# Moving the squares, the row sums and the cast of the high halves from VectorE to ScalarE in the last stage of a four-layer graph network

## The chip, the cores and the metric

The kernel runs on one core of a Trainium2 chip. Its time is the device time in microseconds of one execution; the figure used is the median over several executions. The profile is a separate, profiled execution, which takes longer than the others. Engines are named as in the profile: PE is TensorE's matmul, PEld its weight load, DVE is VectorE, ACT is ScalarE, POOL is GpSimd, SP is SyncE; ACTq and SPq are the queues on which ScalarE and SyncE issue DMAs.

## The reference, cut to what matters

The network has 6250 nodes with 128 features and 106250 edges (`src`, `dst`), and four layers, each with a layer norm and a Relu ahead and a residual sum behind. The change lies in the last of them, which is itself three graph layers:

```python
def _l2norm(v):
    n = jnp.linalg.norm(v, axis=-1, keepdims=True)
    return v / jnp.maximum(n, EPS)          # EPS = 1e-12
...
denom = jnp.maximum(cnt, 1.0)               # cnt: edges that end in each node
for i in range(NUM_LAYERS):                 # 3
    msg = x[src]
    agg = jax.ops.segment_sum(msg, dst, num_segments=N) / denom
    agg = _l2norm(agg)
    out = agg @ Wl[i].T + bl[i]
    out = out + _l2norm(x) @ Wr[i].T
    x = jax.nn.relu(out) if i != NUM_LAYERS - 1 else out
```

Each graph layer sums the rows of the neighbours, divides by the in-degree, scales the sum and the node's own row to length one, multiplies both with a 128x128 matrix, and adds.

## The kernel before, in words

The nodes are padded to 49 tiles of 128. At the start the kernel builds the adjacency (how many edges run from a source to a destination) as one byte for each pair in DRAM; a sum over neighbours is then a dense matmul with that matrix. Destinations are handled in 13 blocks of up to 512 nodes (the last has 128).

`aggregate` (lines 262 to 284) makes the sums of one block. For each group of up to four source tiles it loads the bytes (`ra_in`, three buffers, on SyncE's queue), casts them to fp32r into `ra_r` (two buffers in the last stage), and multiplies. The cast is shared: VectorE casts the first two or three source tiles of a group (L274), ScalarE the rest (L276). The features are kept as a high and a low fp32r half, so each source tile takes two matmuls (L279). The features stand in `cur` (fp32, called `rh` in the profile) and in `cur2` and `other` (both halves, written in turn by alternate layers).

The stage before the last walks over the edges. While it runs, it also sums most of the source tiles for the first graph layer (L1071), into `part`; for that layer, l=0, only the last 5 of 49 source tiles are left to the last stage (`late`). Layers l=1 and l=2 sum all 49.

The last stage (lines 1163 to 1233) loops over l and the 13 blocks. For each block:

- The sum is copied out of PSUM: L1184 on ScalarE, or L1186 on VectorE for l=0, where `part` is added. This gives `ag` (`rag`), features by nodes.
- L1188 squares it on VectorE into `sq` (`rsq`, one buffer). `transposed` makes `hT` (`rhT`) from the node's own rows by four transposes (L291) and a copy on ScalarE (L292).
- For each of the four node tiles there are three small matmuls: L1196 sums the squares over the features, L1197 multiplies `ag` with `Wl`, L1198 `hT` with `Wr`. In the profile each counts as two.
- `n1` (L1201, L1202) and `rsqrt_clipped` (clip L252 on VectorE, Sqrt L254 on ScalarE, reciprocal L255 on VectorE) give the factor `s1` of the aggregate (L1205).
- L1207 and L1209, both on VectorE, square the block's own rows into `r` (`rr`, one buffer) and sum each row into `n2`; this depends on nothing else in the block. `rsqrt_clipped` gives `s2`.
- L1213, L1215, L1217 and L1219 form the output `o` on VectorE, with `r` used again for the second product.
- For l=0 and l=1, L1221 writes Relu(o) to `cur`; `split_halves` then casts it into the high half (L259) and subtracts that for the low half (L260), all on VectorE. For l=2 the residual `rxb` is added (L1226) and the rows are stored; the load of `rxb` (L1225) and the store (L1229) are issued on ScalarE's queue.

No order is written out by hand. A scheduler orders the instructions of each engine when the kernel is built, from priorities that follow the program and from its own estimate of when operands are ready; on the chip each engine then runs its queue in that order. TensorE's queue may therefore hold matmuls of the next block's sum ahead of the small matmuls of this one.

Of the kernel before, what the change touches and what calls it, by code (L numbers as in the profile page):

```python
# [14 lines left out]
AF = mybir.ActivationFunctionType  # L15
ALU = mybir.AluOpType
AX = mybir.AxisListType
# [39 lines left out]
def blk_tiles(b):  # L57
    return min(4, NT - 4 * b)
# [17 lines left out]
def bcast_rows(ap, off, n):  # L76
    return bass.AP(tensor=ap.tensor, offset=ap.offset + off, ap=[[0, P], [1, n]])
# [56 lines left out]
def regular_path(ctx: ExitStack, tc: tile.TileContext, i: dict, out: bass.AP):  # L134

    nc = tc.nc
# [112 lines left out]
    def rsqrt_clipped(dst, n2, n):  # L249

        c = small.tile([P, 4], F32, name="rrq_c")
        nc.vector.tensor_scalar(c[:, :n], n2, 1e-24, None, op0=ALU.max)  # L252
        s = small.tile([P, 4], F32, name="rrq_s")
        nc.scalar.activation(s[:, :n], c[:, :n], AF.Sqrt)  # L254
        nc.vector.reciprocal(dst, s[:, :n])  # L255

    def split_halves(hi, lo, x):

        nc.vector.tensor_copy(hi, x)  # L259
        nc.vector.tensor_tensor(lo, x, hi, ALU.subtract)  # L260

    def aggregate(b, pool, psum, rows2, t0, bufs, extra=(), act=False):


        w = blk_tiles(b) * P
        ps = psum.tile([P, BW], F32, tag="agg", name="ragg1")
        for n, g in enumerate(range(t0, NT, AG1)):
            c = min(AG1, NT - g)
            a = pool.tile([P, AG1, BW], U8, name="ra_in", tag="a_in", bufs=3)
            nc.sync.dma_start(a[:, :c], adj_v[b][:, g:g + c, :])  # L270
            ar = pool.tile([P, AG1, BW], F32R, name="ra_r", tag="a_r", bufs=bufs)
            m = 0 if act else min(2 + n % 2, c)
            if m:
                nc.vector.tensor_copy(ar[:, :m, :w], a[:, :m, :w])  # L274
            if m < c:
                nc.scalar.copy(ar[:, m:c, :w], a[:, m:c, :w])  # L276
            for k in range(c):
                for s in range(2):
                    nc.tensor.matmul(ps[:, :w], rows2[:, s, g + k, :], ar[:, k, :w], start=(g + k == t0 and s == 0),  # L279
                                     stop=(not extra and g + k == NT - 1 and s == 1))  # L280
        for k, (lhs, rhs) in enumerate(extra):
            for s in range(3):
                nc.tensor.matmul(ps[:, :w], lhs[:, s, :], rhs, start=False, stop=(k == len(extra) - 1 and s == 2))
        return ps, w

    def transposed(dst, rows, b, psum):

        nt = blk_tiles(b)
        p = psum.tile([P, 4, P], F32, tag="mm", name="rtr")
        for k in range(nt):  # L290
            nc.tensor.transpose(p[:, k, :], rows[:, 4 * b + k, :], ident)  # L291
        nc.scalar.copy(dst[:, :nt * P], p[:, :nt, :].rearrange("p t d -> p (t d)"))  # L292
# [9 lines left out]
    with ExitStack() as prep:  # L302
# [187 lines left out]
        def mm_tile(shape, name):  # L490
            return ps_m.tile(shape, F32, tag="mm", name=name)

        for b in reversed(range(NBLK)):
            nt = blk_tiles(b)
            ts = slice(4 * b, 4 * b + nt)
            w = nt * P
# [52 lines left out]
            ag = lp.tile([P, BW], F32, name="rag", bufs=1)  # L549
# [8 lines left out]
            r = lp.tile([P, 4, D], F32, name="rr0", bufs=1)  # L558
# [456 lines left out]
    cur = h2  # L1015
# [147 lines left out]
    with tc.tile_pool(name="rl3", reuse_waits="tile", bufs=2) as lp, \  # L1163
            tc.tile_pool(name="ps_a3", reuse_waits="tile", bufs=2, space=bass.MemoryType.PSUM) as ps_a, \
            tc.tile_pool(name="ps_m3", reuse_waits="tile", bufs=6, space=bass.MemoryType.PSUM) as ps_m:
        def mm_tile(shape, name):
            return ps_m.tile(shape, F32, tag="mm", name=name)

        other = lp.tile([P, 2, NT, D], F32R, name="other", bufs=1)
        wlr = lp.tile([P, NL, 2, D], F32, name="rwlr", bufs=1)  # L1170
        nc.scalar.dma_start(wlr[:, :, 0, :], i["Wl_t"].rearrange("l k o -> k l o"))
        nc.scalar.dma_start(wlr[:, :, 1, :], i["Wr_t"].rearrange("l k o -> k l o"))
        blb = lp.tile([P, NL, D], F32, name="rblb", bufs=1)
        nc.scalar.dma_start(blb.rearrange("p l d -> p (l d)"), bcast_rows(i["L3_gnn_bl"], 0, NL * D))
        for l in range(NL):
            final = l == NL - 1
            new2 = other
            for b in range(NBLK):
                nt = blk_tiles(b)
                ts = slice(4 * b, 4 * b + nt)  # L1180
                ps, w = aggregate(b, lp, ps_a, cur2, 0 if l else late, 2)
                ag = lp.tile([P, BW], F32, name="rag3")
                if l:
                    nc.scalar.copy(ag[:, :w], ps[:, :w])  # L1184
                else:
                    nc.vector.tensor_tensor(ag[:, :w], ps[:, :w], part[:, b, :w], ALU.add)  # L1186
                sq = lp.tile([P, BW], F32, name="rsq3", bufs=1)
                nc.vector.tensor_tensor(sq[:, :w], ag[:, :w], ag[:, :w], ALU.mult)  # L1188
                hT = lp.tile([P, BW], F32, name="rhT3")
                transposed(hT, cur, b, ps_m)  # L1190
                pn = mm_tile([P, 4], "rpn3")
                p1 = mm_tile([P, 4, D], "rp13")
                p2_ = mm_tile([P, 4, D], "rp23")
                for t in range(nt):
                    tl = slice(t * P, (t + 1) * P)
                    nc.tensor.matmul(pn[:, t:t + 1], sq[:, tl], ones[:, 0:1], start=True, stop=True)  # L1196
                    nc.tensor.matmul(p1[:, t, :], ag[:, tl], wlr[:, l, 0, :], start=True, stop=True)  # L1197
                    nc.tensor.matmul(p2_[:, t, :], hT[:, tl], wlr[:, l, 1, :], start=True, stop=True)  # L1198

                n1 = small.tile([P, 4], F32, name="rn1")  # L1200
                nc.vector.tensor_tensor(n1[:, :nt], pn[:, :nt], inv_r[:, ts], ALU.mult)  # L1201
                nc.vector.tensor_tensor(n1[:, :nt], n1[:, :nt], inv_r[:, ts], ALU.mult)  # L1202
                s1 = small.tile([P, 4], F32, name="rs1")
                rsqrt_clipped(s1[:, :nt], n1[:, :nt], nt)
                nc.vector.tensor_tensor(s1[:, :nt], s1[:, :nt], inv_r[:, ts], ALU.mult)  # L1205
                r = lp.tile([P, 4, D], F32, name="rr3", bufs=1)
                nc.vector.tensor_tensor(r[:, :nt], cur[:, ts, :], cur[:, ts, :], ALU.mult)  # L1207
                n2 = small.tile([P, 4], F32, name="rn2")
                nc.vector.tensor_reduce(n2[:, :nt], r[:, :nt], AX.X, ALU.add)  # L1209
                s2 = small.tile([P, 4], F32, name="rs2")  # L1210
                rsqrt_clipped(s2[:, :nt], n2[:, :nt], nt)
                o = lp.tile([P, 4, D], F32, name="ro3")
                nc.vector.tensor_tensor(o[:, :nt], p1[:, :nt],  # L1213
                                        s1[:, :nt][:, :, None].to_broadcast([P, nt, D]), ALU.mult)
                nc.vector.tensor_tensor(o[:, :nt], o[:, :nt],  # L1215
                                        blb[:, l, None, :].to_broadcast([P, nt, D]), ALU.add)
                nc.vector.tensor_tensor(r[:, :nt], p2_[:, :nt],  # L1217
                                        s2[:, :nt][:, :, None].to_broadcast([P, nt, D]), ALU.mult)
                nc.vector.tensor_tensor(o[:, :nt], o[:, :nt], r[:, :nt], ALU.add)  # L1219
                if not final:  # L1220
                    nc.vector.tensor_scalar(cur[:, ts, :], o[:, :nt], 0.0, None, op0=ALU.max)  # L1221
                    split_halves(new2[:, 0, ts], new2[:, 1, ts], cur[:, ts, :])
                    continue
                xb = lp.tile([P, 4, D], F32, name="rxb3", bufs=1)
                nc.scalar.dma_start(xb[:, :nt], rows_of(x_d[0], 4 * b, nt))  # L1225
                nc.vector.tensor_tensor(o[:, :nt], o[:, :nt], xb[:, :nt], ALU.add)  # L1226
                full = nt if 4 * b + nt < NT else nt - 1
                if full:
                    nc.scalar.dma_start(rows_of(out, 4 * b, full), o[:, :full])  # L1229
                if full < nt:  # L1230
                    rest = N - (NT - 1) * P
                    nc.scalar.dma_start(out[(NT - 1) * P:N, :], o[:rest, full, :])
            cur2, other = new2, cur2
# [701 lines left out]
```

## Time and profile before

| | us |
|---|---|
| median of 3 runs | 6230.38 |
| the 3 runs | 6239.7, 6225.37, 6230.38 |
| the profiled execution | 7351.81 |
| its span | 7350.0 |
| last stage in it, from about | 6556 |
| of it l=0, l=1, l=2 | 119, 337, 329 |

The span runs from the first to the last instruction of the profiled execution. The stages are cut where the matmuls of a new layer begin. "Granted clock" is the clock that TensorE was allowed, as a share of full speed. In a group of instructions, "128x512 f32<-128x512 f32" is the shape written and the shape read, partitions by elements, and "x36" the count; only the 12 full blocks of each layer have 512 columns. The idle time after the second bar is what the engine spent just before these instructions, with what ended it.

### The profile page before, as it was taken

To read this page: it belongs to the slowest core of one execution; us is meant where nothing else is said; L and a number is where in the kernel's file an instruction comes from. 1 tells how busy PE (TensorE), PEld (TensorE's weight loads), DVE (VectorE), ACT (ScalarE), POOL (GpSimd) and SP (SyncE) were. 2 spreads that over 40 slices of the span, in tenths; PEclk is the share of its full clock that TensorE was granted. 3 is DMA by queue.
4 is the path that set the end of the run, shared out by engine and by line. 5 is a ranking of instruction groups with operands and counts; after the bars stand their busy time and mean duration, and the time that the engine had idled before them with its cause. 6 is when DMAs were issued, how large, how long until landed. Compare 5 with 4: busy or idle time off the path is not lost. (4 is left out here: it accounts for less than half of the span.)

```text
span 7350.0 us, 84003 instructions
## 1 busy us (share of the span) xinstructions
PE 5164.2 (70%) x28067; PEld 4057.3 (55%) x28091; DVE 3328.9 (45%) x7950; ACT 2421.1 (33%) x5478; POOL 2580.9 (35%) x2376
## 2 busy tenths in 40 slices
PE   0010004999899898999869999974466665679999
PEld 0010002666677566888558887654344454557888
DVE  5222203888654113333113332125565656576655
ACT  0100001544433222221222221234456565653443
POOL 6777773000122441111360112453555555520000
PEclk9999999999898998998889998987677677789999
DMA  6210001355444544332564333475445454533444
GB/s 213 73 24 15 0 0 24 104 176 171 128 147 142 124 85 124 92 100 82 117 119 125 96 96 108 88 156 150 112 132 143 129 144 129 147 102 96 125 141 138
DMA packets 605659, 811.78 MB, mean 110 GB/s; under 512 B 116102, under 2 KB 402616, under 8 KB 605084
## 3 DMA queue, kind: packets, MB, share of 16 engines
q1 hardware_dynamic: 372740, 549.03, 24.8%
q0 software_dynamic: 132896, 194.37, 12.1%
q10 hardware_dynamic: 99448, 61.48, 3.3%
q8 instruction: 267, 4.37, 0.3%
q14 instruction: 308, 2.52, 0.1%
HBM read 594.70 MB, written 209.89 MB: 109 GB/s over the span
## 5 line engine op out<-in xcount | busy, mean ns | idle before, releaser
L792 PE MATMUL ragg<-ra_r,r 128*128 128x512 f32 (+1 forms) x6370 | 1548.3, 404 | 10.3 <-ACT r L762 9.4
L792 PEld LDWEIGHTS ragg<-ra_r,r 128*128 128x128 f32 x6370 | 1225.5, 203 | 262.5 <-ACT r L762 10.2
L1113 POOL DMA_INDIRECT rss<-rtab_s,rsrc_c x832 | 807.1, 970 | 799.8 <-DVE mv L1140 470.6
L459 POOL DMA_INDIRECT adj<-rcnt,ixs x832 | 873.9, 1050 | 291.4 <-issue 260.6
L728 POOL DMA_INDIRECT list_d<-rx,rpli x294 | 313.2, 1065 | 1517.9 <-issue 1372.2
L276 ACT CAST ra_r<-ra_in 128x1024 fp32r<-128x1024 uint8 (+3 forms) x494 | 548.5, 1115 | 846.8 <-PE ragg L279 412.5
L279 PE MATMUL ragg<-ra_r,h 128*128 128x512 f32 (+1 forms) x1274 | 446.1, 440 | 526.4 <-ACT h L487 346.4
L786 DVE CAST ra_r<-ra_in 128x1536 fp32r<-128x1536 uint8 (+4 forms) x507 | 388.0, 768 | 917.1 <-PE ragg L792 782.5
L867 POOL DMA_INDIRECT hf_d<-ry,rto x352 | 548.5, 1558 | 583.7 <-DVE ry L853 424.0
L788 ACT CAST ra_r<-ra_in 128x1024 fp32r<-128x1024 uint8 (+3 forms) x468 | 371.8, 797 | 1141.7 <-PE ragg L792 694.2
L517 PE MATMUL ct<-ohd,oht 128*128 128x128 bf16 (+12 forms) x4096 | 351.1, 217 | 512.2 <-remote 324.0
L517 PEld LDWEIGHTS <-oht 128*128 128x128 bf16 x4096 | 220.8, 101 | 663.4 <-remote 324.9
L1146 PE MATMUL acc<-mv,oh 128*128 128x258 f32 x1648 | 375.5, 376 | 272.2 <-DVE mv L1140 231.2
L279 PEld LDWEIGHTS ragg<-ra_r,h 128*128 128x128 f32 x1274 | 232.4, 204 | 546.9 <-ACT h L487 346.7
L1146 PEld LDWEIGHTS acc<-mv,oh 128*128 128x128 f32 x1648 | 317.8, 261 | 314.6 <-DVE mv L1140 255.3
L1126 PE MATMUL pz<-gw,ohT 128*128 128x128 bf16 x2496 | 266.4, 271 | 265.2 <-DVE rz L1128 129.7
L515 DVE TENSOR_SCALAR oht<-seen,typ_f 128x512 bf16<-128x512 bf16 x1024 | 426.2, 473 | 6.5 <-issue 4.9
L1071 PE MATMUL rpart<-ra_r,cur 128*128 128x512 f32 (+1 forms) x1144 | 354.3, 440 | 105.1 <-ACT ra_r L1068 85.5
L1121 DVE TENSOR_TENSOR oh<-seen,tloc 128x1024 fp32r<-128x1024 f32 x208 | 254.3, 1223 | 308.5 <-remote 181.1
L1126 PEld LDWEIGHTS <-ohT 128*128 128x128 bf16 x2496 | 202.9, 125 | 326.6 <-DVE rz L1128 144.8
L274 DVE CAST ra_r<-ra_in 128x1024 fp32r<-128x1024 uint8 (+4 forms) x364 | 268.4, 743 | 197.5 <-PE ragg L279 174.8
L279 PE MATMUL ragg<-ra_r,cur 128*128 128x512 f32 (+1 forms) x1404 | 334.6, 397 | 7.3 <-DVE ra_r L274 6.8
(310 smaller groups left out, 8303.2 us busy)
## 6 DMA issues: line engine op xcount, KB each, us to landing
ra_in<-adj SPq DMA_DIRECT2D x1092, 256.0 KB
row<-list_d SPq DMA_DIRECT2D x111, 516.0 KB
list_d<-rzero SPq DMA_DIRECT2D x65, 774.0 KB
adj<-rzero SPq DMA_DIRECT2D x52, 784.0 KB
rd_b<-dst SPq DMA_DIRECT2D x208, 128.0 KB
gw<-rtab_d SPq DMA_DIRECT2D x208, 96.0 KB
adj<-rcnt,ixs POOLq DMA_INDIRECT x832
rss<-rtab_s,rsrc_c POOLq DMA_INDIRECT x832
```

Of the source, the lines that this page charges most:

```text
L276: nc.scalar.copy(ar[:, m:c, :w], a[:, m:c, :w])
L279: nc.tensor.matmul(ps[:, :w], rows2[:, s, g + k, :], ar[:, k, :w], start=(g + k == t0 and s == 0), stop=(not extra and g + k == NT - 1 and ...
L459: d = nc.gpsimd.indirect_dma_start(out=adj[0:(hi + 1) * ABS], out_offset=bass.IndirectOffsetOnAxis(ap=ixs[:, s, j:j + 1], axis=0), in_=cnt ...
L515: nc.vector.tensor_scalar(oht[:, k, :], iota_t, typ_f[:, c:c + 1], None, op0=ALU.is_equal)
L517: nc.tensor.matmul(ct[:, q, lo:hi], oht[:, k, q * P:(q + 1) * P], ohd[:, k, off:off + hi - lo], start=(n == 0 and k == 0), stop=(n == len( ...
L786: nc.vector.tensor_copy(ar[:, :m, :w], a[:, :m, :w])
L788: nc.scalar.copy(ar[:, m:c, :w], a[:, m:c, :w])
L792: nc.tensor.matmul(ps[:, h_, :w], r2[:, s, g + k, h_ * P:(h_ + 1) * P], ar[:, k, :w], start=(n == 0 and k == 0 and s == 0), stop=(n == len ...
L867: d = nc.gpsimd.indirect_dma_start(out=hf_d[:], out_offset=bass.IndirectOffsetOnAxis(ap=to[:, t:t + 1], axis=0), in_=y[:, t, :], in_offset ...
L1113: nc.gpsimd.indirect_dma_start(out=ss[:, k, 1:], out_offset=None, in_=tab_s[:], in_offset=bass.IndirectOffsetOnAxis(ap=src_c[:, g * WG + k ...
L1126: nc.tensor.matmul(pz[:, k, :], ohT[:, k, :], gw[:, s, :], start=(s == 0), stop=(s == 2))
L1146: nc.tensor.matmul(acc[t], oh[:, k, n * P:(n + 1) * P], mv[:, k].rearrange("p s f -> p (s f)"), start=(g == ends[t][0] and k == 0), stop=( ...
```

## The change

Five lines of the last stage change; nothing else does.

- The squares of the aggregate (L1188) are made by a ScalarE activation.
- The product and the sum over the rows (L1207 and L1209) become one ScalarE activation for each of the block's node tiles, Square with an accumulated sum. It still writes `r`, and its sums go to `n2`.
- For l=0 and l=1 ScalarE writes the high half straight from `o`, as Relu with the output rounded to fp32r. VectorE still writes `cur` with its own Relu, and subtracts the high half for the low one. The cast in `split_halves` is no longer used here.

From L1207 on, the line numbers of the changed kernel shift by up to one.

```diff
                 sq = lp.tile([P, BW], F32, name="rsq3", bufs=1)
-                nc.vector.tensor_tensor(sq[:, :w], ag[:, :w], ag[:, :w], ALU.mult)
+                nc.scalar.activation(sq[:, :w], ag[:, :w], AF.Square)
...
                 r = lp.tile([P, 4, D], F32, name="rr3", bufs=1)
-                nc.vector.tensor_tensor(r[:, :nt], cur[:, ts, :], cur[:, ts, :], ALU.mult)
                 n2 = small.tile([P, 4], F32, name="rn2")
-                nc.vector.tensor_reduce(n2[:, :nt], r[:, :nt], AX.X, ALU.add)
+                for t in range(nt):
+                    nc.scalar.activation(r[:, t], cur[:, 4 * b + t, :], AF.Square, accum_out=n2[:, t:t + 1])
...
                 if not final:
+                    nc.scalar.activation(new2[:, 0, ts], o[:, :nt], AF.Relu)
                     nc.vector.tensor_scalar(cur[:, ts, :], o[:, :nt], 0.0, None, op0=ALU.max)
-                    split_halves(new2[:, 0, ts], new2[:, 1, ts], cur[:, ts, :])
+                    nc.vector.tensor_tensor(new2[:, 1, ts], cur[:, ts, :], new2[:, 0, ts], ALU.subtract)
                     continue
```

## The prediction

> **What bounds the kernel now.** The change touches only the last stage, so I first cut the execution into its stages (busy time by stretch). Columns: us, then busy us of PE, PEld, DVE, ACT and POOL, each with its instructions, granted TensorE clock, DMA share, GB/s.
>
> ```profile
> 6556.00:6675.00 119.00, 90.20 (x475) 77.83 (x475) 94.53 (x251) 25.77 (x55) 0.00 (x0) 0.80 0.18 51
> 6675.00:7012.00 337.00, 333.21 (x1617) 277.81 (x1616) 207.25 (x397) 139.08 (x209) 0.00 (x0) 0.97 0.44 126
> 7012.00:7341.00 329.00, 326.98 (x1610) 276.17 (x1608) 196.33 (x361) 136.43 (x204) 0.00 (x0) 0.97 0.49 143
> ```
>
> These are layers l=0, 1 and 2. In l=1 and l=2 TensorE is busy 99% of the time: there only new waits can matter. In l=0, where a block has 5 source tiles to sum instead of 49, VectorE is busy 79%, ScalarE 22%, TensorE 76%, at a clock of 0.80. The waits of PE and then of PEld in l=0 say what TensorE lacks (us in total, times, longest):
>
> ```profile
> PE rpn L1196 <- DVE rsq L1188: 23.1, 10, 5.4
> PE ragg L279 <- DVE ra_r L274: 5.2, 3, 4.6
> PEld rpn L1196 <- DVE rsq L1188: 26.7, 11, 5.8
> ```
>
> So 23.1 of its 28.6 us of waits are for the square of the aggregates, a VectorE instruction queued behind other VectorE work. In l=1 the same view gives PEld 10.6 us of waits for the VectorE casts, in l=2 4.9 us. The timeline shows the price of one such gap, and what it does to the clock:
>
> ```profile
> 6583.26 0.73 PE L279 MATMUL ragg<-ra_r,cur 128*128 128x512 f32 x2 [0.27 <-DVE ra_r L274]
> 6589.35 0.59 PE L1196 MATMUL rpn<-rones,rsq 128*128 128x1 f32 x2 [5.36 <-DVE rsq L1188]
> 6589.80 0.77 PE L1197 MATMUL rp<-rwlr,rag 128*128 128x128 f32 x2
> ...
> 6655.51 0.38 PE L1196 MATMUL rpn<-rones,rsq 128*128 128x1 f32 x2 [1.66 <-DVE rsq L1188]
> ...
> 6656.77 0.64 PE L1198 MATMUL rp<-rwlr,rhT 128*128 128x128 f32 x2
> ```
>
> A pair of L1198 takes 0.39 us at full clock and 0.64 at half. The groups by shape give the durations (count | busy us, mean ns | idle before):
>
> ```profile
> L1188 DVE TENSOR_TENSOR rsq<-rag 128x512 f32<-128x512 f32 x36 | 24.7, 687 | 0.4 <-ACT rag L1184 0.4
> L1207 DVE TENSOR_TENSOR rr<-rh 128x512 f32<-128x512 f32 x36 | 24.6, 683 | 0.0
> L1209 DVE TENSOR_REDUCE rn<-rr 128x4 f32<-128x512 f32 x36 | 24.4, 677 | 0.4
> L276 ACT CAST ra_r<-ra_in 128x512 fp32r<-128x512 uint8 x144 | 89.7, 623 | 93.1 <-PE ragg L279 84.3 <-DVE rh L1221 8.4 <-DMA ra_in<-adj 0.2
> L1184 ACT COPY rag<-ragg 128x512 f32<-128x512 f32 x24 | 13.9, 580 | 0.0
> ```
>
> **What leaves VectorE, what arrives on ScalarE.** A full block loses 0.69 (L1188), 0.68 (L1207), 0.68 (L1209) and, in l=0 and 1, the cast of the high halves (L259, 0.42): 2.47 us. ScalarE gains a square and a Relu of 512 columns, which have no row; the nearest are 0.58 (copy from PSUM) and 0.62 (cast from SBUF), and I take 0.62. The row sums become four 128-column squares with an accumulator; the same form stands in the stage before (L241: 0.294 us, starts 0.30 apart, and 0.186 for the read of the accumulator): 4 x 0.30 + 0.19 = 1.39 us. Together 2.6 us a block. No table load comes: the built order has no load after the Sqrt of L243, as before. No DMA is added; in l=2 the store of `ro3` (0.38 us) and the load of `rxb3` (0.53) stay on ScalarE's queue, now with squares between them.
>
> [...]
>
> **Layer l=0, worked out.** Before, the first L1196 of the stage starts at 6567.3 and that of the last block at 6672.5: 105.2 us for 12 steps, 8.77 each. After, VectorE's own work is (94.5 / 13 = 7.3) - 2.5 = 4.8 us a block, ScalarE's 2.0 + 2.6 = 4.6, TensorE's at full clock 10 x 0.226 (L279) + 4 x 0.67 (L1196 to L1198) + 0.36 (L291) = 5.3. None of these sums is the step, since blocks hand over between engines. I walked the built order with these durations.
> - TensorE's loop: for most later blocks the order has all ten L279, four transposes, then the twelve small matmuls. After the last L279: 0.1 + 0.65 for L1186 on VectorE, 0.1 + 0.62 for the square on ScalarE, 2.7 for the small matmuls, 2.3 for the next L279, 0.2 for hand-overs: 6.7. Where part of the next block's L279 stands ahead of the small ones, 5.2 to 5.6.
> - The loop through `rr3` (one buffer): L1219 frees it; Relu 0.6, four squares 1.4, clip, Sqrt and reciprocal 0.5, L1217, L1186 and L1219 at 0.6 each and the small ones: 4.6 to 5. It is shorter, so it doesn't set the step. Queued behind the Relu, which waits for L1219, are the squares, a cast, the copy of `rhT3` and the next square; the walk puts the square 0.1 to 0.7 us behind its aggregate.
> - Walking blocks 0 to 4 gives steps of 6.9, 5.2, 6.9 and 6.7 us; mean with the later form 6.7. Gain: 12 x (8.77 - 6.7) = 25 us. At the head, two VectorE instructions fewer before the first casts: 0.5 us, which I leave in the range.
>
> [...] The walk has gaps of 0 to 1.3 us. [...] A block at half clock costs 4 x (1.28 - 0.67) = 2.4 us for its small matmuls. I take one to two such blocks left, +3: l=0 gains 22.
>
> **Layers l=1 and l=2.** In the chain of waits the L279 of a block follow the block before by 26.0 us in l=1 (6777.32 to 6803.35) and 25.6 in l=2 (7189.81 to 7215.40). In l=1 the difference is VectorE being late with a cast when L1221, L1207, L259, L260 and L1209 stand between casts; two of these and L1207 go. L260 now waits for ScalarE's Relu, with the next L274 behind it: in the walk the Relu ends 0.3 us after VectorE is ready, and the cast still ends 0.35 us before TensorE needs it. Gain 12 x 0.35 = 4 us. Against it, ScalarE: the square comes after L1184 and L292 (0.48 us each to the next), so `rsq3` is ready at 1.6 us after the copy starts against 1.3 on VectorE. The built order now puts all eight L279 of the next block's first group (1.81 us) ahead of L1196, not seven, and its end covers nearly all; I put 0.1 us on each of 24 blocks, +2. Then the casts of ScalarE: a group of four source tiles lasts 8 x 0.226 = 1.81 us on TensorE, there are two buffers, and VectorE casts the first tiles, so ScalarE's part is first needed 0.9 or 1.36 us into its group. Its slack is 1.81 + 0.9 - 1.05 = 1.7 or 1.81 + 1.36 - 0.62 = 2.5 us. The Relu and two squares (1.4 us) stand ahead of one cast, two squares (0.8) ahead of the next; in l=2 three squares (1.1) and the store, then one square and the load. All are below the slack; the tightest is the load in l=2, which would leave 0.3 us where it takes 1.69 (once before). I put 0, covered by TensorE's other buffer; without that cover, it is the second rival.
>
> **Sum.** -22 - 4 + 2 = -24 us against the profiled execution's own 7351.8 us (span 7350.0). The runs have a median of 6230.4, 1121 us less; no trace shows where. The last stage is set by TensorE at full clock and by instructions of fixed length, so I carry the difference over in us: 6230.4 - 24 = 6206.
>
> **Rivals.**
> - *ScalarE's waits take the place of VectorE's in l=0.* For it: the queue is in order, and the Relu, a square and a Sqrt there wait each for another VectorE instruction; a turn lost per block costs some 1.4 us. Against it: ScalarE would be 65 to 70% busy only. Then the step is 8.1, the gain 8 us, l=1's is eaten by the late square: 6224, which the measurement (about 0.2%, 12.5 us) can't tell from none.
> - *ScalarE's casts come late in l=1 and l=2: slower.* Its place is the cast behind the Relu and squares, and in l=2 behind the store and load. For it: L276 has 0.76 to 1.2 us of idle time before each cast, and 1.4 us of new work goes there; TensorE has nothing else to do. Against it: VectorE's tiles come first in each group. It decides from 1.0 us of stall a block (24 us, which cancels the gain); at 1.8 us, the price where the whole slack of a group is lost, it is 43 us: 6230 - 24 + 43 = 6249.
> - *TensorE becomes the bound of l=0*, with its 5.3 to 5.6 us steps and full clock: 12 x 3.3 = 40 us, and 4 in l=1: 6187.
>
> That the change doesn't do what it says is excluded by the built order: all five edits are in the stage's three layers.
>
> **How the numbers follow.** Forecast 0.60, TensorE-bound 0.08, both faster; ScalarE's waits 0.19, the same; late casts 0.13, slower. The range runs from 6187 (TensorE-bound) to 6230 (the rival of l=0 with no gain at all); outside it are the late casts and a little below. Faster 0.68, same 0.19, slower 0.13.
>
> **What would show it.** Right: l=0 takes 93 to 100 us instead of 119; the waits of L1196 are then for ScalarE's L1188 and below 14 us in total; granted clock above 0.88; the step of l=1 falls to 25.6 to 25.8; ACT in l=0 at 55 us or more. Wrong: waits of L279 for ACT L276 over 10 us in l=1 or l=2 (late casts); a step in l=0 above 8 us with ScalarE idle for VectorE and VectorE for ScalarE.

## The result, and the profile after

| | before | after |
|---|---|---|
| median, us | 6232.33 | 6194.34 |
| lowest to highest of 4 runs each | 6225.37 to 6239.7 | 6178.78 to 6197.05 |
| the profiled execution | 7351.81 | 6197.05 |
| last stage in it | 789.3 | 751.1 |

The ratio after to before is 0.9936, with a 95% interval of 0.9923 to 0.9949: 38 us less. The profiled execution of before is some 1120 us above its other runs (that of after is one of its four), and the excess stands ahead of the last stage, which begins at 6560.7 us of the trace before and at 5444.1 after. The two last stages differ by 38.2 us, as much as the medians do, so all that is compared below lies in the last stage. From here on the stage is cut by matmuls of L279: l=0 runs from the first that reads `cur` to the first that reads `other`, l=1 to the last that reads `other`, l=2 to the last that reads `cur`. The rest is what follows the sums of the last block.

| us | l=0 | l=1 | l=2 | rest | sum |
|---|---|---|---|---|---|
| before | 114.0 | 333.3 | 332.6 | 9.4 | 789.3 |
| after | 79.8 | 327.2 | 334.4 | 9.7 | 751.1 |

Nine tenths of the gain lies in l=0. The three stretches of the changed kernel, cut as the prediction cuts those of before: busy time by stretch (us, then busy us of PE, PEld, DVE, ACT and POOL, each with its instructions, granted clock, DMA share, GB/s):

```profile
5440.00:5524.00 84.00, 71.10 (x464) 61.40 (x464) 65.65 (x189) 49.90 (x162) 0.00 (x0) 0.95 0.25 72
5524.00:5851.00 327.00, 324.96 (x1615) 273.36 (x1615) 184.49 (x350) 165.56 (x345) 0.00 (x0) 0.98 0.44 128
5851.00:6186.00 335.00, 331.26 (x1621) 277.85 (x1620) 177.15 (x326) 159.02 (x321) 0.00 (x0) 0.97 0.49 142
```

In the exact cut of l=0 VectorE has some 27 us less to do, ScalarE 24 more, and TensorE itself is busy 19 us less: its clock is 0.98 there (0.95 with the head of the stretch), where it was 0.81. What TensorE waits for in l=0 (us in total, times, longest):

```profile
PEld rpn L1196 <- ACT rsq L1188: 10.8, 10, 1.7
PE rpn L1196 <- ACT rsq L1188: 7.9, 7, 1.5
...
PE ragg L279 <- DVE ra_r L274: 5.1, 3, 4.2
```

The wait for the square fell from 23.1 to 7.9 us, and is now for ScalarE. The one long wait for VectorE (4.2 us) is at the head. Two lines of TensorE's timeline show a gap like those before, and what stands behind it:

```profile
5485.48 0.38 PE L1196 MATMUL rpn<-rones,rsq 128*128 128x1 f32 x2 [1.49 <-ACT rsq L1188]
...
5486.03 0.39 PE L1198 MATMUL rp<-rwlr,rhT 128*128 128x128 f32 x2
```

The longest gap left for the square is 1.49 us, and the pair of L1198 takes 0.39 us after it, full clock. The new ScalarE groups by shape (count | busy us, mean ns | idle before):

```profile
L1209 ACT ACTIVATE rr<-rh 128x128 f32<-128x128 f32 x147 | 43.5, 297 | 2.3 <-DVE ro L1219 2.3
L1209 ACT ACTIVATION_READ_ACCUMULATOR rr<-rh 128x1 f32 x147 | 27.5, 187 | 0.0
L1188 ACT ACTIVATE rsq<-rag 128x512 f32<-128x512 f32 x36 | 23.0, 638 | 2.9 <-PE rpn L1196 1.5 <-DVE rag L1186 1.4
L1221 ACT ACTIVATE other<-ro 128x512 fp32r<-128x512 f32 x12 | 7.5, 628 | 3.9 <-DVE ro L1219 3.9
```

These are the durations that the prediction took from neighbours (0.62 for both wide ones, 0.294 and 0.186 for the sums).

### The profile page after: what moved, and what is told of

It reads as the page before. It is cut to its first block, busy times and chain, and to the rows that moved or that the text cites. A ratio compares the mean times of both kernels' runs of the same rounds, so it can differ in the third digit from the quotient of the medians.

```text
span 6195.2 us, 84249 instructions
## 1 busy us (share of the span) xinstructions
PE 5068.4 (82%) x28067; PEld 3980.5 (64%) x28091; DVE 3220.4 (52%) x7807; ACT 2488.0 (40%) x5837; POOL 2522.1 (41%) x2376
## 3 DMA queue, kind: packets, MB, share of 16 engines
q14 instruction: 310, 2.54, 0.2%
## 5 line engine op out<-in xcount | busy, mean ns | idle before, releaser
L459 POOL DMA_INDIRECT adj<-rcnt,ixs x832 | 811.4, 975 | 278.2 <-issue 241.8
L276 ACT CAST ra_r<-ra_in 128x1024 fp32r<-128x1024 uint8 (+3 forms) x494 | 545.1, 1114 | 804.3 <-PE ragg L279 377.0
L279 PE MATMUL ragg<-ra_r,h 128*128 128x512 f32 (+1 forms) x1274 | 438.0, 435 | 145.2 <-ACT ra_r L276 145.1
L1146 PE MATMUL acc<-mv,oh 128*128 128x258 f32 x1648 | 356.6, 361 | 109.9 <-DVE mv L1140 108.1
L274 DVE CAST ra_r<-ra_in 128x1024 fp32r<-128x1024 uint8 (+4 forms) x364 | 268.6, 744 | 252.8 <-PE ragg L279 239.3
L1146 PEld LDWEIGHTS acc<-mv,oh 128*128 128x128 f32 x1648 | 299.3, 245 | 149.1 <-DVE mv L1140 141.8
L1071 PE MATMUL rpart<-ra_r,cur 128*128 128x512 f32 (+1 forms) x1144 | 326.1, 412 | 46.9 <-ACT ra_r L1068 40.6
L279 PE MATMUL ragg<-ra_r,cur 128*128 128x512 f32 (+1 forms) x1404 | 330.8, 394 | 7.7 <-DVE ra_r L274 7.7
L820 DVE COPY at<-rtr 128x512 f32<-128x512 f32 x112 | 77.1, 688 | 494.0 <-PE rtr L819 494.0
L279 PEld LDWEIGHTS ragg<-ra_r,h 128*128 128x128 f32 x1274 | 228.8, 201 | 163.2 <-ACT ra_r L276 146.0
L851 PE MATMUL rp<-st,rsh 128*128 128x256 f32 x1344 | 314.0, 382 | 9.6 <-DVE ry L853 9.6
```

What stands on the lines that cost most here:

```text
L459: d = nc.gpsimd.indirect_dma_start(out=adj[0:(hi + 1) * ABS], out_offset=bass.IndirectOffsetOnAxis(ap=ixs[:, s, j:j + 1], axis=0), in_=cnt ...
L1071: nc.tensor.matmul(ps[:, :w], cur2[:, s, g + k, :], ar[:, k, :w], start=(g + k == t0 and s == 0), stop=(g + k == t1 - 1 and s == 1))
L1146: nc.tensor.matmul(acc[t], oh[:, k, n * P:(n + 1) * P], mv[:, k].rearrange("p s f -> p (s f)"), start=(g == ends[t][0] and k == 0), stop=( ...
```

## The experiments

Two theories of l=0 stood first. A: what counts is VectorE's work, all of it; the wait shows up at L1196 only because the square happens to stand there, and each part of the change pays by what it takes off VectorE. B: what counts is the square's place behind other work in VectorE's queue; moving it alone frees TensorE. A third, C, came with the later runs: since the change, ScalarE's order or TensorE sets the step. All times below are of the profiled executions and the exact cut; the lengths of l=0 in kernels with the same code for it differ by 4.6 us at a low clock (before 113.9 at 0.81, `l12_only` 109.3 at 0.86) and by 1.6 at a high one (after 79.8 at 0.98, `l0_only` 81.5 at 0.95). Less than that is not told apart in one trace.

### One part at a time

`p_square`:

```diff
-                nc.vector.tensor_tensor(sq[:, :w], ag[:, :w], ag[:, :w], ALU.mult)
+                nc.scalar.activation(sq[:, :w], ag[:, :w], AF.Square)
```

> Only the square of the aggregates (L1188) goes to ScalarE; row sums and high halves stay on VectorE. Measure: l=0, from its first L279 to the first L279 of l=1, 113.9 us before and 79.8 with the whole change. Theory A (VectorE's load counts, whatever leaves it): 0.69 of the 2.47 us a block leave, so about 28% of the 34 us: l=0 at 104. Theory B (what counts is that the square, on TensorE's path, no longer queues on VectorE): most of the gain, l=0 at 90 or less, and waits of L1196 below 10 us. Total: A -10 us, B -25 us.

`p_rowsum`:

```diff
-                nc.vector.tensor_tensor(r[:, :nt], cur[:, ts, :], cur[:, ts, :], ALU.mult)
-                nc.vector.tensor_reduce(n2[:, :nt], r[:, :nt], AX.X, ALU.add)
+                for t in range(nt):
+                    nc.scalar.activation(r[:, t], cur[:, 4 * b + t, :], AF.Square, accum_out=n2[:, t:t + 1])
```

> Only the row sums (L1207, L1209) go to ScalarE. Theory A (load): 1.36 of 2.47 us a block, 55% of the 34 us: l=0 at 95. Theory B (the square's place in the queue): the square still stands behind L1213 to L1219 on VectorE; l=0 at 106 or more, with the waits of L1196 for DVE still above 15 us. Total: A -19 us, B -8 us or less.

`p_high`:

```diff
+                    nc.scalar.activation(new2[:, 0, ts], o[:, :nt], AF.Relu)
                     nc.vector.tensor_scalar(cur[:, ts, :], o[:, :nt], 0.0, None, op0=ALU.max)
-                    split_halves(new2[:, 0, ts], new2[:, 1, ts], cur[:, ts, :])
+                    nc.vector.tensor_tensor(new2[:, 1, ts], cur[:, ts, :], new2[:, 0, ts], ALU.subtract)
```

> Only the high halves (L1221, L259) go to ScalarE. Theory A (load): 0.42 of 2.47 us a block, 17%: l=0 at 108. Theory B: l=0 at 112 to 116, no gain. In both l=1 may lose or gain 2 us: VectorE has one cast less there, but L260 waits for ScalarE's Relu. Total: A -6 us, B 0.

Measured, with the ratio to before and its 95% interval:

| kernel | VectorE busy in l=0, us | TensorE busy in l=0, us | l=0, us | last stage, us | ratio |
|---|---|---|---|---|---|
| before | 91.1 | 89.8 | 114.0 | 789.3 | |
| `p_square` | 82.4 (-8.7) | 84.5 | 102.4 (-11.6) | 774.4 | 0.999 [0.9981, 0.9998] |
| `p_rowsum` | 73.7 (-17.4) | 79.9 | 92.4 (-21.6) | 765.4 | 0.9964 [0.995, 0.9978] |
| `p_high` | 87.1 (-4.0) | 88.3 | 110.6 (-3.4) | 786.9 | 1.0001 [0.9992, 1.001] |
| after | 63.6 (-27.5) | 71.0 | 79.8 (-34.2) | 751.1 | 0.9936 [0.9923, 0.9949] |

The three parts of l=0 add up to 36.6 us, the whole is 34.2, and each pays about 1.2 us for a microsecond taken off VectorE (the high half 0.85, but its 3.4 us are less than one trace can tell, and its runs show no gain). The square, whose wait was the largest row of before, brings a third. The waits of TensorE in l=0 of `p_square` show why:

```profile
PE ragg L279 <- DVE ra_r L274: 16.7, 12, 4.6
PE rpn L1196 <- ACT rsq L1188: 5.8, 4, 2.5
```

The wait did not vanish with the square; it moved to the next thing that TensorE wants of the same engine, the cast L274 (16.7 us in 12 times, where before had 5.2 in 3). `p_rowsum` leaves the square on VectorE and cuts its wait from 23.1 to 7.9 us. That fits A, and not B. A trace is one execution, though, and the medians differ from such comparisons by up to 9 us: `p_square` is 6 us below before in its runs (1 to 12 by the interval) and 15 by the last stage of its trace; for `p_rowsum` the two are 22 and 24. By the medians the three parts bring 6, 22 and -3 us, 25 in all, against 38 for the whole; the intervals are too wide to tell whether the parts gain something only together.

### Where the gain lies: by layer

`l0_only` has the whole change where `l == 0` and the code of before elsewhere; `l12_only` the reverse. Each edit takes this form:

```diff
-                nc.vector.tensor_tensor(sq[:, :w], ag[:, :w], ag[:, :w], ALU.mult)
+                if l == 0:
+                    nc.scalar.activation(sq[:, :w], ag[:, :w], AF.Square)
+                else:
+                    nc.vector.tensor_tensor(sq[:, :w], ag[:, :w], ag[:, :w], ALU.mult)
```

> The whole change in l=0, the kernel before in l=1 and l=2. If the gain is made in l=0 alone, l=0 takes 80 us and l=1 333 (as before), total -32 to -35 us. If l=1's share of 6 us is real, this kernel is 4 to 6 us slower than the whole change, which the traces' stage lengths can show and the times hardly. If the seam between l=0 and l=1 needs the change in l=1 too, l=0 takes 84 to 86.

> The change in l=1 and l=2 only, the kernel before in l=0. If l=1's gain of 6 us is due to VectorE's casts being in time there, l=1 is at 327 to 329 (333.3 before) and l=0 at 114; l=2 at 331 to 335, as TensorE is the bound. Total -4 us, inside what the measurement can tell. If l=1's gain came from the seam with l=0 (the last block of l=0 done behind the first sums of l=1), l=1 stays at 332 to 334.

Measured: `l0_only` 0.9938 [0.9921, 0.9955], with l=0 at 81.5 us, l=1 at 332.3, l=2 at 330.3. `l12_only` 0.9998 [0.9988, 1.0007], with 109.3 (the clock), 328.8 and 334.9. So the change in l=1 gains some 4 to 6 us and in l=2 loses some 2 to 4, and nearly the whole difference that the runs can tell is l=0.

### Is it the clock? Filler matmuls

`clock_fill` is the kernel before with six more matmuls in each block of l=0, whose result is thrown away, to keep TensorE from idling.

```diff
+            for _ in range(fill if n == 0 else 0):
+                nc.tensor.matmul(ps[:, :w], rows2[:, 0, g, :], ar[:, 0, :w], start=True, stop=True)
...
-                ps, w = aggregate(b, lp, ps_a, cur2, 0 if l else late, 2)
+                ps, w = aggregate(b, lp, ps_a, cur2, 0 if l else late, 2, fill=0 if l else 6)
```

> The kernel before with six more matmuls of 128x512 ahead of each block's sum in l=0 (their result is overwritten by the sum that starts after them): TensorE has 6 x 0.226 = 1.36 us more to do in each of 12 blocks, and is idle less. It asks whether the low clock of l=0 (0.81 before, 0.98 after) is a cause of its length or only goes with it. Theory A (VectorE's load sets the step): the fillers lie in TensorE's waits, the clock rises above 0.9, and l=0 stays within 110 to 117 us (114.0 before). Theory C (the half clock cost what TensorE's busy time lost, 90 to 71 us): with a full clock l=0 shortens to 100 or less. If the fillers simply add up, l=0 is 130.

Measured: 1.0001 [0.9992, 1.001]. Its l=0, busy time by stretch:

```profile
5457.40:5570.60 113.20, 99.76 (x552) 87.56 (x552) 92.16 (x240) 22.52 (x49) 0.00 (x0) 0.86 0.16 46
```

TensorE is busy 10 us longer, and the layer is as long as before (113.2 against 114.0): what the fillers add is made up for elsewhere. But the clock rose only to 0.86, not above 0.9 as expected, so this run does not show that a low clock costs nothing. Other traces show that it costs. Here are before, `l12_only`, which has the code of before in l=0, and after, in the exact cut of l=0:

```profile
6560.75:6674.68 113.93, 89.77 (x473) 77.51 (x474) 91.04 (x240) 22.20 (x49) 0.00 (x0) 0.81 0.15 45
5445.55:5554.90 109.35, 85.36 (x474) 73.12 (x474) 91.01 (x240) 22.21 (x49) 0.00 (x0) 0.86 0.16 47
5444.06:5523.90 79.84, 71.01 (x463) 61.30 (x463) 63.67 (x183) 46.05 (x155) 0.00 (x0) 0.98 0.22 66
```

With VectorE's work the same, `l12_only` is 4.6 us shorter than before, and TensorE's busy time is 4.4 us shorter: its matmuls are faster, and the layer gains it. `l0_only` and after have the same code in l=0 too and differ in the same way, by 1.6 us in length and 1.8 in busy time, at 0.95 and 0.98. From before to after TensorE's idle time falls by 15.3 us (24.2 to 8.8) and its busy time by 18.8. The granted clock is 1.0 or 0.5 in every clock record of before and after, with half clock for 42 us of l=0 before and 4 after; the mean of 0.86 in `l12_only`, taken the same way, gives 31. At the price that the first two show (4.6 us for 11.5), some 15 us of the 34 come by way of the clock; this is an estimate. This is no rival of A, since each of TensorE's six waits of 1.66 us or more for the square in l=0 of before has half clock behind it (see the last section), but it is the second way in which such a wait costs, and may be why a microsecond off VectorE pays more than one. A good clock is not needed for a gain: `p_square` gains 11.6 us at 0.83.

### More off VectorE, and more onto it

If A holds without end, the next microsecond off VectorE should pay too. `pool_low` gives the low half of l=0 to GpSimd, which does nothing else there:

```diff
-                    nc.vector.tensor_tensor(new2[:, 1, ts], cur[:, ts, :], new2[:, 0, ts], ALU.subtract)
+                    (nc.vector if l else nc.gpsimd).tensor_tensor(new2[:, 1, ts], cur[:, ts, :], new2[:, 0, ts], ALU.subtract)
```

> The changed kernel, with the subtraction that makes the low half in l=0 (L1223) on GpSimd, which is idle in the last stage. VectorE loses another 0.68 us in each of 12 full blocks. Theory A (in all six kernels so far VectorE is busy 78 to 80% of l=0): 55.5 us of work over 0.8 is 69, but TensorE's own 13 x 5.3 with the slow start is 71 to 72: l=0 at 72 to 74, total -6 us against the change. Theory B (the square's way, L1186 to L1188 to L1196, sets it now): l=0 stays at 79 to 81. If GpSimd and VectorE get into each other's way, the VectorE rows get longer and l=0 rises.

Measured: 0.9948 [0.9932, 0.9964]; l=0 takes 84.5 us, 4.7 more than after. VectorE's busy time did not fall by the 7 us of the ten subtractions that lie in l=0 of after but rose from 63.6 to 67.2. The row of its wide cast in l=0, of `pool_low`:

```profile
L274 DVE CAST ra_r<-ra_in 128x1024 fp32r<-128x1024 uint8 x12 | 15.1, 1260 | 6.5 <-PE ragg L279 5.1 <-ACT rrq_s L254 0.9 <-ACT other L1221 0.5
```

and of after:

```profile
L274 DVE CAST ra_r<-ra_in 128x1024 fp32r<-128x1024 uint8 x12 | 8.2, 684 | 4.8 <-PE ragg L279 4.8
```

A cast takes 1260 ns instead of 684. Two lines of the timeline of `pool_low` show what it stands beside:

```profile
5475.76 1.27 POOL L1223 TENSOR_TENSOR other<-rh,other 128x512 fp32r<-128x512 f32 x1 [4.65 <-ACT other L1221]
...
5475.79 1.79 DVE L274 CAST ra_r<-ra_in 128x1024 fp32r<-128x1024 uint8 x1 [0.23 <-ACT rrq_s L254]
```

The cast starts 0.03 us after GpSimd's subtraction, ends 0.55 us after that one's end and takes 1.79 us. Two more that start 0.02 and 0.03 us after a subtraction, at 5489.52 and 5496.74, take 1.80 and 1.79; one that starts 0.89 us after it, at 5483.17, takes 0.95. All four end 0.54 or 0.55 us after the subtraction beside them; the cause is not shown. So this run is no test of A.

The next two are. `cast1_act` moves the cast of the single-tile group of l=0 (L274, 128x512) to ScalarE; `dve_more` adds a product that nothing reads to VectorE.

```diff
-            m = 0 if act else min(2 + n % 2, c)
+            m = 0 if act or (one and c == 1) else min(2 + n % 2, c)
...
-                ps, w = aggregate(b, lp, ps_a, cur2, 0 if l else late, 2)
+                ps, w = aggregate(b, lp, ps_a, cur2, 0 if l else late, 2, one=not l)
```

> The changed kernel, with the cast of the single-tile group of each full block of l=0 (L274, 128x512, 0.42 us on VectorE) moved to ScalarE (L276, 0.62). Theory A (VectorE's work sets the step of l=0, at a busy share of about 0.80 in every kernel so far): VectorE has 63.6 - 12 x 0.42 = 58.6 us, l=0 takes 58.6 / 0.80 = 73 us instead of 79.8, and the kernel is 6 to 7 us faster than the change. Theory C (since the change, ScalarE's order or TensorE sets the step): ScalarE has 46 + 12 x 0.62 = 53.4 us, l=0 stays at 79 to 82, or grows, with waits of L279 for ACT L276.

```diff
+                if l == 0:
+                    more = lp.tile([P, 4, D], BF16, name="rmore", bufs=1)
+                    nc.vector.tensor_tensor(more[:, :nt], cur[:, ts, :], cur[:, ts, :], ALU.mult)
                 for t in range(nt):
```

> The changed kernel, with one more product of the block's own rows on VectorE in each block of l=0 (128x512, where L1207 stood, into a bf16 tile of its own that nothing reads), 0.69 us each. Theory A (VectorE's work sets the step): VectorE has 63.6 + 12.5 x 0.69 = 72 us, l=0 takes 72 / 0.80 = 90 us, 10 more than after. Theory B (only the chain through the square counted, and VectorE has 16 us of idle time in l=0 that takes the product): 80 to 82 us.

Measured: `cast1_act` 0.9949 [0.9932, 0.9965], `dve_more` 0.9948 [0.9932, 0.9965]. The busy time of l=0, first of `cast1_act`:

```profile
5440.20:5519.70 79.50, 72.34 (x463) 63.12 (x463) 58.85 (x166) 52.04 (x168) 0.00 (x0) 0.95 0.23 67
```

then of `dve_more`:

```profile
5430.80:5516.40 85.60, 76.36 (x470) 64.66 (x470) 72.50 (x198) 47.11 (x160) 0.00 (x0) 0.93 0.20 57
```

VectorE has 4.8 us less in `cast1_act`, and the layer is hardly shorter: 79.5 us against 79.8, or 77.9 at the clock of after (in `mix_cast1` below, with the same l=0), where A said 73. With 8.9 us more in `dve_more` it is 5.8 longer, where A said 10 and B nothing. Of these, 3.3 stand in the first step, from block 0 to block 1 (9.95 us against 6.68), whose small matmuls ran at half clock; the ten steps behind it are together only 1.4 us longer (63.74 against 62.36). So A, which held from before to after, ends at the changed kernel, and the share of 80% that VectorE shows in both does not by itself tell the bound: about there it passes to TensorE's own loop. Block 10 of after shows that loop, on VectorE, ScalarE and TensorE:

```profile
5510.64 0.69 DVE L1186 TENSOR_TENSOR rag<-ragg,part 128x512 f32<-128x512 f32 x1 [1.01 <-PE ragg L279]
5511.66 0.63 ACT L1188 ACTIVATE rsq<-rag 128x512 f32<-128x512 f32 x1
5512.34 0.38 PE L1196 MATMUL rpn<-rones,rsq 128*128 128x1 f32 x2 [1.30 <-ACT rsq L1188]
```

VectorE is idle until TensorE's last L279 ends, adds `part` at once, ScalarE squares 0.33 us after that, and TensorE has then waited 1.30 us. In after, TensorE is busy 71.0 of 79.8 us, and of the rest 7.9 are its waits for the square, which a lighter VectorE hardly shortens: in `cast1_act` they are still 6.0. ScalarE, at 65% there, is not the bound either, and TensorE doesn't wait for its casts. In `dve_more` it does, for 5.5 us in 8 times: there ScalarE's casts stand behind a Relu that waits for VectorE. Of C, TensorE's half holds.

### Are ScalarE's casts near their limit in l=1 and l=2?

`act_more` makes each row sum of l=1 and l=2 three times, some 2.3 us more of ScalarE's time in each block.

```diff
-                for t in range(nt):
+                for t in [u for u in range(nt) for _ in range(3 if l else 1)]:
                     nc.scalar.activation(r[:, t], cur[:, 4 * b + t, :], AF.Square, accum_out=n2[:, t:t + 1])
```

> The changed kernel, with each row sum of l=1 and l=2 made three times (the last write counts): ScalarE has 8 x 0.30 = 2.4 us more in each of 24 full blocks. It looks for the price of the rival 'ScalarE's casts come late'. By the slack of the prediction (1.7 us for a cast of two source tiles, 2.5 for one) the order puts two to four squares between casts, below the slack: l=1 and l=2 longer by 0 to 3 us together. If ScalarE's casts were near the edge already, each us added would show: 58 us more.

Measured: 0.9944 [0.9926, 0.9962]. ScalarE's busy time rises from 166.0 to 193.8 us in l=1 and from 158.7 to 186.7 in l=2; the layers take 327.5 and 332.0 us, against 327.2 and 334.4. So ScalarE had some 2.3 us more room in each block than the change used. The run does not test the slack of a single cast: in after and in `act_more` alike, the longest run of other work between two casts of l=1 and l=2 is 1.6 us (L1184, L292 and the square, one behind the other), leaving out the seam to l=0.

### A better version?

`mix` has the change in l=0 and l=1 and the code of before in l=2 (the form of `l0_only`, with `if not final`); `mix_cast1` adds the edit of `cast1_act`.

> The change in l=0 and l=1, the code of before in l=2. If the 2 us that l=2 lost come from the square, the row sums and the store that share ScalarE's queue there: l=2 takes 330 to 333 us instead of 334 to 335, l=0 and l=1 stay at 80 and 327, and the kernel is 2 to 3 us faster than the change. If they come from a drift of the loads of the adjacency, l=2 stays at 334.

> The two before last but one together: the change in l=0 and l=1, the code of before in l=2, and the single-tile cast of l=0 on ScalarE. If both gains hold: l=0 at 73, l=1 327, l=2 331, 9 us below the changed kernel. If neither holds: as the changed kernel, 751 us for the last stage.

Measured on one chip with `cast1_act` and `dve_more`: `mix` 0.9942 [0.9926, 0.9959], `mix_cast1` 0.9938 [0.9922, 0.9955]. In `mix` l=2 takes 331.1 us, in `mix_cast1` 332.5; in seven traces with the square of l=2 on VectorE (these two, before, `p_rowsum`, `p_high`, `l0_only` and `clock_fill`) it is 330.3 to 333.9, mean 332.0, in seven with it on ScalarE 332.0 to 334.9, mean 333.7. The two ranges overlap. So some 2 us may be had in l=2, too little for the runs to tell. No version is shown to beat the changed kernel; `mix_cast1`, with the shortest l=0 (77.9) and a last stage of 749.0, is level with it.

## Why the prediction was right, and which terms were off

The sign, the place and the mechanism were right; the size was 24 us where 38 were measured. That the two largest terms it left out, the ends of l=0 and of l=1, both fell on the fast side, and inside the range, was luck: it gave no reason for them.

- *The bound before* (VectorE's lateness, read from the rows of L1196): right, though the row names the wrong part of it. VectorE's whole load was late; the square was only what TensorE met first. The prediction counted all four instructions taken off, so its sum did not suffer.
- *The step, 8.77 to 6.7 us*: right in kind. The first L1196 of block 0 and of block 11 are 69.0 us apart after (5450.18 to 5519.21), 6.27 a step, against 8.71 before: 26.8 us over 11 steps, where the walk gives 22.8. The four steps that were walked, at 6.9, 5.2, 6.9 and 6.7, took 6.68, 5.31, 6.62 and 6.37. For the seven behind them the prediction took its longer form, 6.7, throughout: five take 6.87 to 7.11, one 5.70, and one 3.22, where the small matmuls of blocks 4 and 5 follow each other with no sum between them. That one step is most of the difference.
- *The last step of the layer*, counted as one of the twelve at 2.07 us, is the term most off. From L1196 of block 11 to the first L279 of l=1 it took 11.5 us before and 4.7 after: 6.8 us. Block 12, with one tile, has hardly any matmuls to cover VectorE's work, and its own small matmuls now come behind the first sums of l=1.
- *The clock, +3*: too large. In after the gaps left, up to 1.49 us, are followed by pairs of 0.39 us, not 0.64, and the clock of l=0 is 0.98. `l0_only`, with the same code there, has a mean clock of 0.95, some 8 us at half clock against 4, and is 1.6 us longer. In before the gap of 1.66 us ahead of 6655.51 does have half clock behind it, from 6656.67 (see the last section), but after shows none of the one to two such blocks taken: it is at full clock from 5447.72 to the end of l=0.
- These make l=0: 22 + 4.0 (steps) + 4.7 (last step) + 3 (clock) + 0.5 (head, left to the range) = 34.2, the whole of the measured 34.2.
- *l=1, 4 us less, and 1 more for the late square*: 6.1 less. The waits of PEld for the casts of VectorE, 10.1 us with this cut, are 4.9; those for the square rose from 0.7 to 2.5. These rows give 3.4 net. By step, the first ten of the layer fall from 26.00 to 25.64 us, 3.6 in all and as forecast; the last two, at the short block, bring another 2.1 (25.27 and 24.77 before, 25.01 and 22.89 after), which the prediction did not count. `l0_only`, with the code of before in l=1, has 24.87 for the last one, `mix`, with the change, 23.38. The remaining 0.4 stay open.
- *l=2, 1 us more*: 1.8 more. The waits for the square are 2.5 there too, and ScalarE's L276 waits 11.3 us for its adjacency bytes, against 6.6. But these waits do not explain the length: `mix` has 7.6 at 331.1 us, `l0_only` 10.3 at 330.3, `act_more` 1.9 at 332.0. The cause stays open, and the spread of l=2 over the traces is as large as the effect.
- *The casts of ScalarE at no cost*: right. No wait of L279 for L276 is in l=1, 0.3 us in l=2, and `act_more` shows the room. The slack of 1.7 to 2.5 us was not put to the test, since the longest work between two casts is 1.6 us. That work, L1184 and L292 with the square behind them, is longer than the 1.4 us of the Relu and two squares that the prediction put ahead of a cast in l=1, and it did not name it.
- *The exchange, 2.6 us of ScalarE for 2.47 of VectorE*: in engine time the move is about even, as the prediction counted (the square 638 ns against 687 on VectorE, the Relu 628 against 420 for the cast), and that was no reason to keep the work on the engine that the others waited for.

The rival of ScalarE's waits in VectorE's place did not come, though the row of 7.9 us looks like it. Of these, 6.8 stand at blocks 6 and 8 to 11, as in block 10 above: the square starts 0.2 to 0.5 us behind its aggregate, and the wait is TensorE's own loop, which the prediction put at 1.47 us a step (0.1 + 0.65 + 0.1 + 0.62). Only at block 4 does ScalarE's own order cost TensorE something, 0.67 us: the square starts 1.84 us behind its aggregate, after a Relu and four row sums, where the walk said 0.1 to 0.7. The measured 38 us lie nearer to the 44 of the TensorE-bound rival than to the forecast's 24, yet its step of 5.3 to 5.6 was not reached; the ends of l=0 and l=1 made up for it.

Of the signs given, the waits for L1188 (7.9, below 14), the clock, the step of l=1 (25.64) and the absence of late casts came as said. Two did not. l=0 lies far below 93 to 100 us of the old 119-us stretch (84.0 with the head). And ScalarE is busy for 49.9 us, not 55: neighbouring ScalarE instructions overlap by 0.1 us (the 0.63-us square at 5491.89 is followed at 5492.42), and the Relus of the last two blocks fall into l=1.

## What to carry to other kernels

When one engine is late, the wait stands at whatever its consumer needs first (in `p_square`, with the square gone, the waits for the cast L274 rose from 5.2 to 16.7 us): sum all of that engine's work in the stage, and expect a single instruction moved off to bring its share and shift the rest to the next row. The gain per microsecond ends where another loop takes over, so walk that loop (here TensorE's own matmuls and the square behind them) before moving more. A wait costs twice where half clock follows it (some 15 of the 34 us here, by the estimate above), so count its slow matmuls with it. Look at the seam to the next layer by itself: a short last block has little to hide behind, and may gain more than a step (6.8 us here, against 2.4 for a step).

## What the runs showed of the hardware

**Half clock came in pieces of 3.41 us, behind idle time of TensorE.** In and next to l=0 of before, half clock begins at 6544.03, 6588.40, 6615.71, 6625.95, 6643.01, 6656.67 and 6663.49 us and lasts 20.48, 6.83, 3.41, 6.83, 6.83, 3.41 and 13.65 us; in after one stretch lies there, of 20.48 us from 5427.24. All these lengths, and the times from one start to the next, are whole multiples of 3.41 us. Cut at these bounds into pieces of 3.41 us, l=0 of before and of after has 44 pieces that begin in it and have full clock. Of 31 in which TensorE was idle for less than 1.0 us, none is followed by a piece at half clock; of five with 1.66 us or more, all of before, each is; of the eight between, one. The gap of 1.66 us ahead of 6655.51, which the prediction shows, lies whole in one piece, from 6653.25. This sorts l=0 alone: over the whole of before and after, 66 of 2058 pieces at full clock with less than 0.2 us idle are followed by half clock too, for which neither trace shows the reason.

One and the same gap was followed by half clock in one run and by full clock in another. `cast1_act` and `mix_cast1` have the same order in l=0 and both a gap of 1.29 us ahead of block 10's L1196. In `cast1_act`, that gap and the first matmuls behind it, then the piece of 3.41 us that holds the gap, and the next (columns as above):

```profile
5507.25 0.38 PE L1196 MATMUL rpn<-rones,rsq 128*128 128x1 f32 x2 [1.29 <-ACT rsq L1188]
...
5509.15 0.64 PE L1198 MATMUL rp<-rwlr,rhT 128*128 128x128 f32 x2
...
5510.72 3.39 PE L279 MATMUL ragg<-ra_r,cur 128*128 128x512 f32 x10
...
5505.69:5509.10 3.41, 2.12 (x19) 1.88 (x18) 3.41 (x8) 2.96 (x8) 0.00 (x0) 1.00 0.06 17
5509.10:5512.51 3.41, 3.41 (x14) 3.09 (x14) 1.69 (x7) 1.05 (x7) 0.00 (x0) 0.50 0.27 79
```

In `mix_cast1`:

```profile
5501.10 0.38 PE L1199 MATMUL rpn<-rones,rsq 128*128 128x1 f32 x2 [1.29 <-ACT rsq L1189]
...
5503.80 2.54 PE L279 MATMUL ragg<-ra_r,cur 128*128 128x512 f32 x10
...
5499.18:5502.59 3.41, 2.12 (x19) 1.85 (x17) 3.19 (x7) 2.96 (x6) 0.00 (x0) 1.00 0.01 2
5502.59:5506.00 3.41, 3.41 (x23) 3.03 (x23) 2.13 (x9) 1.45 (x11) 0.00 (x0) 1.00 0.34 94
```

With the same queue, the same gap and 2.12 us of busy TensorE in the piece, the clock halves in one run and stays full in the other (ten matmuls in 3.39 and 2.54 us); l=0 takes 79.5 and 77.9 us. Where the gap lies does not settle this pair, since both lie whole in one piece; what does is not shown.

**VectorE's casts took longer beside GpSimd.** The casts of `pool_low` above took up to 1.80 us beside subtractions of some 1.28 us, against a mean of 0.684 in after: an idle third engine was no free place for this work.
